# Batches with 528 slots: the sixteen tail tokens laid twice in each head's 32 rows, one pass for the tail's context

## The chip, the core and the metric

The kernel runs on one core of one Trainium2 chip (trn2). The metric is the device time of one execution in microseconds (us). Before the change the runs took 1044.05 us in the median (three runs: 1043.74, 1044.05 and one of 5687.53 us, which the median leaves out of account).

The core has five engines that run side by side and wait for each other by semaphores: TensorE (PE in the profile; its weight loads are listed apart as PEld), VectorE (DVE), ScalarE (ACT), GpSimd (POOL) and SyncE (SP), which here only issues transfers.

## The reference

One attention layer with a residual, 16 batches of 512 channels by 1024 tokens, 8 heads of 64 channels. Query, key and value are the same projection `q`. `mask` holds 0 or 1 for each token.

```python
xt = jnp.transpose(x, (0, 2, 1))
q = xt @ Wq.T
qh = q.reshape(B, T, NH, dk).transpose(0, 2, 1, 3)
scores = scale * jnp.einsum('bhqd,bhkd->bhqk', qh, qh)
logits = (scores * cmask + (1.0 - cmask) * NEG) * rmask
attn = jax.nn.softmax(logits, axis=-1)
ctx = jnp.einsum('bhqk,bhkd->bhqd', attn, qh)
ctx = ctx.transpose(0, 2, 1, 3).reshape(B, T, D)
out = ctx @ Wo.T
return x + jnp.transpose(out, (0, 2, 1))
```

A token with mask 0 gets no weight as a key (`cmask`), and as a query its logits are all 0 (`rmask`), so that its context is the mean of `q` over all tokens. Only the tokens with mask 1, a little over half of the 1024, need attention among themselves.

## The kernel before

**Slots.** For each batch the kernel puts the tokens with mask 1 into the first of `A` slots and gathers their rows of `x` by an indirect transfer on POOL's queue. `A` is fixed by the batch's rank (L64): 544 for batches 0 to 4, 528 for batches 5 to 13, 512 for the last two; batches 2 to 15 are taken in falling order of their number of such tokens. Slots 0 to 511 are four tiles of 128. What lies above 512 is the tail: 32 slots, 16 slots or none. Empty slots hold zeros, and their share is taken off the softmax sums afterwards.

**Precision by parts.** Values are cut into a high and a low part, and products are formed from the parts: in fp16 for the projections and scores, in fp32r (a reduced format of fp32 that TensorE takes) for the tail's context.

**Query and spread.** `query` (L497) projects into `q`; `qsplit` (L516) cuts a 128-channel chunk, that is two heads, into `hl` (high, low, high again) on DVE and lets SP's queue spread it by four transfers into `xx` (L536 to L539), where the parts of each head lie side by side. `hl` and `xx` are 544 slots wide; where `A` is 528, a memset (L525) puts zeros into the last 16 slots of `hl`.

**Scores and context.** For a head pair (`p`, four of them) and a key tile (`i`, four of them) `scores` (L653) forms the products of the tile's keys with all `A` queries into PSUM, four matmuls (L693) for each of two heads, and ACT takes the exponential into `p` (L697). `attend` (L702) multiplies these by the values `v` and accumulates over the key tiles in one PSUM tile `pav` (L718).

**The tail.** For the keys above 512 four heads share one tile: head `r` of the four lies in rows 32r to 32r+31, one row for each tail slot. `scores` with `i` None (L662 to L687) forms their products (L668), the exponential (L672), a high and a low part of it in fp32r (L677, L678), and spreads these by transfers into `pt`: for a head pair `pt` holds the high parts in 64 rows and the low parts of the same two heads in the other 64. The values come from `tail_copy` (L572), which repeats the tail's slots of `q` for the four row groups in `qt`, and `value_tail` (L580), which transposes `qt`, clears what belongs to the other head, and splits it into high (`t[:, 0]`, L597 on ACT) and low (`t[:, 1]`, L598 on DVE). With 16 tail slots rows 16 to 31 of each group are zero (a memset on POOL, L577, clears them once). `attend` with `i` 4 (L721, L722) then makes two passes over `pav` for each of the two column halves, high values and low values, four matmuls for a head pair. Since `pt` holds the high and the low exponentials in different rows, the two passes form all four products of parts. ACT then copies `pav` to `c` (L726).

**Order.** `run` (L925) writes out a list of steps (`S`: sixteen pairs of `p` and `i`, and two tail scores) for each batch and fills between them, by costs written at each step, the next batch's projection, transposes and values and the last batch's normalization and output projection (L809). A scheduler then orders the instructions of each engine by estimated times and priorities; each engine takes its instructions in that order.

Of the kernel before, what the change touches and what calls it, by code (L numbers as in the profile page):

```python
# [10 lines left out]
F32 = mybir.dt.float32  # L11
F32R = mybir.dt.float32r
F16 = mybir.dt.float16
I32 = mybir.dt.int32
AF = mybir.ActivationFunctionType
ALU = mybir.AluOpType
AX = mybir.AxisListType
PS = bass.MemoryType.PSUM

P = 128  # L20
# [10 lines left out]
C = 544  # L31
CT = C - 512
CQ = C + 2
HG = H // 2
# [12 lines left out]
class Fast:  # L47
# [91 lines left out]
    def setup2(self):  # L139
        nc, fixed = self.nc, self.fixed  # L140

        self.quad = fixed("quad", [P, HG])
        nc.vector.tensor_reduce(self.quad, self.ident.rearrange("p (r t) -> p r t", r=HG), AX.X, ALU.add)
        self.xh = fixed("xh", [P, DC, CQ], F16)
        self.xl = fixed("xl", [P, DC, CQ], F16)
        for t in (self.xh, self.xl):
            nc.gpsimd.memset(t[:, :, C + 1:], 0.0)

        self.rcol = [fixed("rcol%d" % k, [P, P]) for k in range(2)]
        self.smcol = [fixed("smcol%d" % k, [P, P]) for k in range(2)]  # L150
        for t in self.rcol + self.smcol:
            nc.gpsimd.memset(t, 0.0)

        self.two = fixed("two", [P, DK], F16)
        nc.vector.tensor_tensor(self.two, self.ident[:, :DK], self.ident[:, DK:], ALU.add)

        self.big = fixed("big", [P, self.B + 2 * DC])

        self.par = fixed("par", [P, 2])
        nc.vector.tensor_tensor(self.par, self.quad[:, 0:2], self.quad[:, 2:4], ALU.add)  # L160

    def load(self, name, c, half=None, after=None):

        if name not in self.w:
            self.w[name] = tuple(self.fixed("w" + name + k, [P, DC, D], F16) for k in "hl")
        cols = slice(0, D) if half is None else slice(half * D // 2, (half + 1) * D // 2)
        raw = self.sb([P, D], F32, "xa", 13)[:, cols]
        self.once(self.nc.sync.dma_start(out=raw, in_=self.src[name][c * P:(c + 1) * P, cols]), after)
        self.raw[name, c, half] = raw, cols

    def split(self, name, c, half=None):
        nc = self.nc
        raw, cols = self.raw[name, c, half]
        hi, lo = (w[:, c, cols] for w in self.w[name])
        nc.scalar.activation(hi, raw, AF.Copy, scale=SW)
        nc.vector.scalar_tensor_tensor(lo, raw, SW, hi, ALU.mult, ALU.subtract)
# [339 lines left out]
    def qsplit(self, b, e):  # L516


        nc, s = self.nc, self.st[b]
        A = s["A"]  # L520
        S = max(A, C) if A > 512 else A
        q = s["q"][:, e, :A]
        full = self.sb([P, 3, C], F16, "hl", 2)
        if A < S:
            nc.vector.memset(full[:, :, A:], 0.0)  # L525
        hl = full[:, :, :A]
        nc.vector.tensor_copy(hl[:, 0, :], q)
        nc.vector.tensor_tensor(hl[:, 1, :], q, hl[:, 0, :], ALU.subtract)
        nc.vector.tensor_copy(hl[:, 2, :], hl[:, 0, :])
        hl = full[:, :, :S]  # L530
        full = self.sb([P, 4, C], F16, "xx", 5)
        xx = full[:, :, :S]

        def spread():
            lo, up = slice(0, DK), slice(DK, P)
            nc.sync.dma_start(out=xx[lo, 0:2, :], in_=hl[lo, 0:2, :])  # L536
            nc.sync.dma_start(out=xx[up, 0:2, :], in_=hl[lo, 1:3, :])
            nc.sync.dma_start(out=xx[lo, 2:4, :], in_=hl[up, 0:2, :])
            self.last_xx = nc.sync.dma_start(out=xx[up, 2:4, :], in_=hl[up, 1:3, :]).ins  # L539

        self.later(spread)
        s["xx"].append(xx)
# [29 lines left out]
    def tail_copy(self, b, g):  # L572

        s = self.st[b]
        n = s["A"] - 512
        if g == 0 and b and s["A"] < self.wide[b - 1]:
            self.nc.gpsimd.memset(self.qt[:, :, :, n:], 0.0)  # L577
        self.nc.scalar.copy(self.qt[:, :, :, :n], s["q"][:, 2 * g:2 * g + 2, 512:512 + n].unsqueeze(2).broadcast_to([P, 2, HG, n]))

    def value_tail(self, b, g):  # L580


        nc, s = self.nc, self.st[b]
        if g == 0:
            s["vt"] = []
            s["sdt"] = self.sb([P, H], F32, "sdt")
        q = self.qt
        pv = self.pm([P, 2, P])
        for k in range(2):
            nc.tensor.transpose(pv[:, k, :], q[:, k].rearrange("p r t -> p (r t)"), self.ident)  # L590
        v = self.sb([P, HG, DK], F32, "tmp", 2)
        split = lambda t: t.rearrange("p (k h) d -> p k h d", h=2)
        nc.vector.tensor_tensor(split(v), pv.rearrange("p k (h d) -> p k h d", h=2),
                                self.par.unsqueeze(1).unsqueeze(3).broadcast_to([P, 2, 2, DK]), ALU.mult)
        self.squares(v, s["sdt"][:, HG * g:HG * g + HG], g == (b > 0), b == 0)
        t = self.sb([P, 2, HG, DK], F32R, "vt", 3)
        nc.scalar.copy(t[:, 0], v)  # L597
        nc.vector.tensor_tensor(t[:, 1], v, t[:, 0].bitcast(F32), ALU.subtract)  # L598
        s["vt"].append(t)

    def shift(self, b, g):
# [100 lines left out]
    def attend(self, b, p, i, ps):  # L702
        nc, s = self.nc, self.st[b]
        A = s["A"]
        CH = A // 2

        if i == 3:
            s["pav"] = self.ps_av.tile([P, 2, 512], F32, tag="av", name="pav")
        for g in range(2):
            for k in (1, 0) if i < 4 else range(2):  # L710
                cols = slice(g * CH, (g + 1) * CH)
                if i < 4:
                    with ExitStack() as st:
                        if self.group_first:

                            st.enter_context(self.behind(self.group_first))
                            st.enter_context(self.tc.high_priority(offset=HPO))
                        mm = nc.tensor.matmul(s["pav"][k * DK:(k + 1) * DK, g, :CH], lhsT=s["v"][p][:, i, k * DK:(k + 1) * DK],  # L718
                                              rhs=ps[k][:, cols], start=(i == 3), stop=(i == 0 and A == 512))
                    self.group_first = self.group_first or mm.ins  # L720
                elif A > 512:  # L721
                    nc.tensor.matmul(s["pav"][:, g, :CH], lhsT=s["vt"][p // 2][:, k, p % 2 * 2:p % 2 * 2 + 2, :],  # L722
                                     rhs=s["pt"][:, p % 2, cols], start=False, stop=(k == 1))
        if i == 4:
            c = self.sb([P, C], F32, "c", 4)
            nc.scalar.copy(c[:, :A].rearrange("p (g c) -> p g c", g=2), s["pav"][:, :, :CH])  # L726
            s["c"].append(c)
# [197 lines left out]
    def run(self, flag):  # L925
        B = self.B
        L = lambda f, *a: lambda: f(*a)
        S = [(p, i) for p in range(NP) for i in range(4)]
        S.insert(2, (0, None))
        S.insert(13, (1, None))  # L930
        N = len(S)
# [363 lines left out]
```

## Time and profile before

| what | value |
|---|---|
| median of the runs | 1044.05 us |
| the profiled execution's own time | 1045.58 us |
| its span (first to last instruction) | 1043.8 us |
| mean granted TensorE clock | 0.995 |
| exponentials of the 528-slot batches (5 to 13) | from about 350 us to about 912 us |

The profile is of one execution. A group's "busy" is the time in which at least one instruction of the group ran; matmuls overlap each other, so busy divided by the count is less than the mean duration of one. "Idle before" is the time that the engine sat idle right before instructions of the group, with what ended it. In the timeline, rows are merged runs of like instructions: the first column is the start, the second the length.

### The profile page before, as it was taken

The numbers are of one execution on the slowest core, as the hardware profiler recorded it, in microseconds if no ns is written. First come the engines' busy times: TensorE is split into PE (matmuls) and PEld (weight loads), VectorE is DVE, ScalarE is ACT, GpSimd is POOL, SyncE is SP. The second block draws the span as 40 slices with busy tenths as digits, with TensorE's granted clock in tenths as the row PEclk, the third lists the DMA queues.
The fourth block names the chain that finished last, engine by engine and source line by source line (L and its number), as shares of the span: only waits on it lengthen the run. The fifth ranks groups of instructions, "written<-read, shape, count | busy, mean of one in ns | idle before, by whom it ended". The sixth has DMA issues, their size and how long they took to land. (4 is left out here: it accounts for less than half of the span.)

```text
span 1043.8 us, 23675 instructions
## 1 busy us (share of the span) xinstructions
PE 994.7 (95%) x8527; PEld 692.3 (66%) x8527; DVE 720.9 (69%) x2408; ACT 656.4 (63%) x1702; POOL 299.5 (29%) x308
## 2 busy tenths in 40 slices
PE   7798999999999999999999999999999999999995
PEld 6576667666666766667676666766767676776552
DVE  7897668666766657767666777667678675756562
ACT  5876666666666665757666557665766666655650
POOL 3101023223301222233222223223333322325652
PEclk9899999999999999999999999999999999999999
DMA  6756555557645576666558656565665566546641
GB/s 212 215 142 175 138 152 166 164 156 207 189 125 149 135 214 176 166 189 163 164 159 233 183 141 188 152 192 175 202 193 153 164 172 183 154 132 195 201 170 74
DMA packets 78796, 177.74 MB, mean 170 GB/s; under 512 B 14688, under 2 KB 20576, under 8 KB 78672
## 3 DMA queue, kind: packets, MB, share of 16 engines
q1 hardware_dynamic: 57584, 108.40, 38.3%
q0 software_dynamic: 21088, 67.75, 20.7%
q8 instruction: 70, 1.15, 0.5%
q14 instruction: 54, 0.44, 0.1%
HBM read 91.49 MB, written 33.91 MB: 120 GB/s over the span
## 5 line engine op out<-in xcount | busy, mean ns | idle before, releaser
L697 ACT ACTIVATE p<-pss,nm 128x528 f32<-128x528 f32 (+2 forms) x512 | 359.9, 707 | 190.6 <-PE pss L693 181.1
L693 PE MATMUL pss<-xx 128*128 128x264 f16 (+2 forms) x2048 | 302.7, 277 | 8.2 <-ACT p L697 7.0
L718 PE MATMUL pav<-p,v 128*64 128x264 f32 (+2 forms) x2048 | 243.3, 390 | 0.0
L693 PEld LDWEIGHTS <-xx 128*128 128x128 f16 x2048 | 195.0, 99 | 63.9 <-issue 26.8
L718 PEld LDWEIGHTS pav<-p,v 128*64 128x64 f32 x2048 | 141.4, 137 | 85.7 <-issue 13.3
L893 POOL DMA_INDIRECT y_out<-xa,idx x68 | 73.7, 1083 | 284.7 <-PE pss L693 129.4
L508 PE MATMUL pm<-xh,wqh 128*128 128x264 f16 (+5 forms) x512 | 142.4, 278 | 4.1 <-DVE xa L814 2.3
L508 PE MATMUL pm<-xl,wqh 128*128 128x264 f16 (+5 forms) x512 | 141.7, 277 | 0.2 <-DVE xl L440 0.2
L508 PE MATMUL pm<-xh,wql 128*128 128x264 f16 (+5 forms) x512 | 141.9, 277 | 0.0
L390 POOL DMA_INDIRECT xa<-x_in,idx x68 | 67.9, 998 | 203.1 <-PE pss L693 89.6
L508 PEld LDWEIGHTS <-wqh 128*128 128x128 f16 x1024 | 98.1, 99 | 24.5 <-issue 7.5
L697 ACT ACTIVATION_READ_ACCUMULATOR p<-pss,nm 128x1 f32 x512 | 104.1, 203 | 0.0
L893 POOL DMA_INDIRECT y_out<-xi,idx x60 | 71.5, 1192 | 101.4 <-PE pss L693 38.1
L809 PE MATMUL pm<-woh,ch 128*128 128x512 f16 x240 | 91.1, 379 | 0.0
L809 PE MATMUL pm<-woh,cl 128*128 128x512 f16 x240 | 90.9, 379 | 0.0
L809 PE MATMUL pm<-wol,ch 128*128 128x512 f16 x240 | 90.9, 379 | 0.0
L390 POOL DMA_INDIRECT xi<-x_in,idx x60 | 61.7, 1029 | 97.3 <-PE pss L693 33.8
L511 ACT ACTIVATE q<-pm 128x264 f32<-128x264 f32 (+5 forms) x128 | 50.3, 393 | 60.1 <-PE pm L508 59.8
L809 PEld LDWEIGHTS <-ch 128*128 128x128 f16 x480 | 45.9, 98 | 44.7 <-issue 0.9
L814 DVE SCALAR_TENSOR_TENSOR xa<-pm,xa 128x512 f32<-128x512 f32 x60 | 41.3, 688 | 44.3 <-PE pm L809 40.6
L880 DVE TENSOR_TENSOR xi<-xi,ub 128x512 f32<-128x512 f32 (+1 forms) x60 | 40.7, 687 | 44.2 <-PE pss L693 41.7
L791 DVE TENSOR_TENSOR c<-c,rb 128x528 f32<-128x528 f32 (+2 forms) x64 | 45.4, 710 | 32.8 <-PE pm L508 16.3
(220 smaller groups left out, 1511.4 us busy)
## 6 DMA issues: line engine op xcount, KB each, us to landing
xx<-hl SPq DMA_DIRECT2D x224, 136.0 KB
xm<-x_nat_in SPq DMA_DIRECT2D x56, 512.0 KB
rb<-rd SPq DMA_DIRECT2D x72, 132.0 KB
rb<-rd SPq DMA_DIRECT2D x40, 136.0 KB
pt<-c SPq DMA_DIRECT2D x36, 132.0 KB
pt<-p SPq DMA_DIRECT2D x36, 132.0 KB
ub<-ud SPq DMA_DIRECT2D x16, 256.0 KB
xx<-hl SPq DMA_DIRECT2D x32, 128.0 KB
```

The source lines that it names most:

```text
L390: dma = self.nc.gpsimd.indirect_dma_start(out=tile[:n], out_offset=None, in_=self.x, in_offset=bass.IndirectOffsetOnAxis(ap=idx, axis=0))
L508: self.beat = nc.tensor.matmul(pq, lhsT=w[:, c, e * P:(e + 1) * P], rhs=xx[:, c, cols], start=(k == 0), stop=(k == 3 * DC - 1)).ins
L511: nc.scalar.activation(s["q"][:, e, cols], pq, AF.Copy, scale=1.0 / (SX * SW))
L693: self.beat = nc.tensor.matmul(pt[:, g, :CH], lhsT=xx[:, 2 * k, i * P:(i + 1) * P], rhs=xx[:, 2 * k + a, g * CH:(g + 1) * CH], start=(a == ...
L697: self.exp = [nc.scalar.activation(t.rearrange("p (g c) -> p g c", g=2), pt[:, :, :CH], AF.Exp, bias=s["nm"][p // HG][:, p % HG:p % HG + 1 ...
L718: mm = nc.tensor.matmul(s["pav"][k * DK:(k + 1) * DK, g, :CH], lhsT=s["v"][p][:, i, k * DK:(k + 1) * DK], rhs=ps[k][:, cols], start=(i == ...
L791: self.once(nc.vector.tensor_tensor(c[:, :A], c[:, :A], s["rb"][p], ALU.mult), self.beat if p < 3 else None)
L809: nc.tensor.matmul(po[:cols.stop - cols.start], lhsT=a[:, e, cols], rhs=w[:, e, :], start=(e == 0 and k == 0), stop=(e == DC - 1 and k == 2))
L814: self.nc.vector.scalar_tensor_tensor(x, po, 1.0 / (SX * SW), x, ALU.mult, ALU.add)
L880: self.once(self.nc.vector.tensor_tensor(x[:n], x[:n], s["ub"][:n], ALU.add), self.beat)
L893: dma = self.nc.gpsimd.indirect_dma_start(out=self.out, out_offset=bass.IndirectOffsetOnAxis(ap=idx, axis=0), in_=x, in_offset=None)
```

## The change

In batches with 528 slots the tail's 16 tokens are laid twice in each head's 32 rows, where the second 16 rows held zeros.

- `setup2` makes two columns of constants on DVE, once: `low`, which is 1 in the second half of every 32 rows and else 0, and `sign`, which is -1 there and else 1.
- `qsplit` copies slots 512 to 527 of `hl` to slots 528 to 543, after the three instructions that fill `hl`, in place of the memset ahead of them.
- `tail_copy` fills all of `qt`, eight repeats of 16 slots in place of four, and needs no memset on POOL.
- `value_tail` puts the high part, with `sign`, into `t[:, 1]`, and into `t[:, 0]` the high part in the first copy's rows and the low part in the second copy's.
- `attend` makes one pass with `t[:, 0]` in place of two: two matmuls for a head pair in place of four.

Batches with 544 and 512 slots keep their instructions.

```diff
@@ setup2
+        self.low = fixed("low", [P, 1])
+        nc.vector.tensor_reduce(self.low, self.ident.rearrange("p (r k t) -> p k r t", r=HG, k=2)[:, 1], AX.XY, ALU.add)
+        self.sign = fixed("sign", [P, 1])
+        nc.vector.tensor_scalar(self.sign, self.low, -2.0, 1.0, ALU.mult, ALU.add)
@@ qsplit
-        S = max(A, C) if A > 512 else A
         q = s["q"][:, e, :A]
         full = self.sb([P, 3, C], F16, "hl", 2)
-        if A < S:
-            nc.vector.memset(full[:, :, A:], 0.0)
         hl = full[:, :, :A]
         nc.vector.tensor_copy(hl[:, 0, :], q)
         nc.vector.tensor_tensor(hl[:, 1, :], q, hl[:, 0, :], ALU.subtract)
         nc.vector.tensor_copy(hl[:, 2, :], hl[:, 0, :])
-        hl = full[:, :, :S]
-        full = self.sb([P, 4, C], F16, "xx", 5)
-        xx = full[:, :, :S]
+        S = C if A > 512 else A
+        if A < S:
+            nc.vector.tensor_copy(full[:, :, A:], full[:, :, 512:A])
+            hl = full
+        xx = self.sb([P, 4, C], F16, "xx", 5)[:, :, :S]
@@ tail_copy
-        if g == 0 and b and s["A"] < self.wide[b - 1]:
-            self.nc.gpsimd.memset(self.qt[:, :, :, n:], 0.0)
-        self.nc.scalar.copy(self.qt[:, :, :, :n], s["q"][:, 2 * g:2 * g + 2, 512:512 + n].unsqueeze(2).broadcast_to([P, 2, HG, n]))
+        r = P // n
+        self.nc.scalar.copy(self.qt.rearrange("p k r t -> p k (r t)").rearrange("p k (r t) -> p k r t", t=n),
+                            s["q"][:, 2 * g:2 * g + 2, 512:512 + n].unsqueeze(2).broadcast_to([P, 2, r, n]))
@@ value_tail
-        nc.scalar.copy(t[:, 0], v)
-        nc.vector.tensor_tensor(t[:, 1], v, t[:, 0].bitcast(F32), ALU.subtract)
+        if s["A"] == C:
+            nc.scalar.copy(t[:, 0], v)
+            nc.vector.tensor_tensor(t[:, 1], v, t[:, 0].bitcast(F32), ALU.subtract)
+        else:
+            nc.scalar.activation(t[:, 1], v, AF.Copy, scale=self.sign)
+            nc.vector.scalar_tensor_tensor(t[:, 0], v, self.low, t[:, 1].bitcast(F32), ALU.mult, ALU.add)
@@ attend
-            for k in (1, 0) if i < 4 else range(2):
+            for k in (1, 0) if i < 4 else range(2 if A == C else 1):
...
-                                     rhs=s["pt"][:, p % 2, cols], start=False, stop=(k == 1))
+                                     rhs=s["pt"][:, p % 2, cols], start=False, stop=(k == 1 or A < C))
```

## The prediction

> **What bounds the kernel now.** I read the page first: the busy shares and the clock.
>
> ```profile
> span 1043.8 us, 23675 instructions
> PE 994.7 (95%) x8527; PEld 692.3 (66%) x8527; DVE 720.9 (69%) x2408; ACT 656.4 (63%) x1702; POOL 299.5 (29%) x308
> PE   7798999999999999999999999999999999999995
> PEclk9899999999999999999999999999999999999999
> ```
>
> TensorE is busy 95% of the span, and from the fifth slice to the last but one 90% or more of each; the next engine has 69%. A busy TensorE may still be waiting inside its pipeline, so I looked next at who waits for whom: the page's costliest groups and the table of waits.
>
> ```profile
> L697 ACT ACTIVATE p<-pss,nm 128x528 f32<-128x528 f32 (+2 forms) x512 | 359.9, 707 | 190.6 <-PE pss L693 181.1
> L693 PE MATMUL pss<-xx 128*128 128x264 f16 (+2 forms) x2048 | 302.7, 277 | 8.2 <-ACT p L697 7.0
> PE pss L693 <- ACT p L697: 7.0, 15, 0.8
> ```
>
> ScalarE's exponentials wait 181.1 us for TensorE's scores; the scores wait 7.0 us for the exponentials, never over 0.8 us at once. The wait lies on ScalarE's side, so TensorE's stream sets the pace. The changed batches run from about 350 to 912 us; a table by windows of 90 us, from which the first row and the sum of six, shows this stage alone.
>
> ```profile
> 380.00:470.00 90.00, 87.77 (x776) 61.05 (x775) 67.26 (x239) 56.41 (x146) 27.05 (x26) 1.00 0.62 177
> sum 540.00, PE 526.72 PEld 369.76 DVE 384.13 ACT 347.80 POOL 160.06; mean PE 87.79 PEld 61.63 DVE 64.02 ACT 57.97 POOL 26.68
> ```
>
> The granted clock there is 1.00. TensorE is busy 526.72 of 540 us (97.5%), VectorE 384.13 (71%), ScalarE 347.80 (64%). What leaves TensorE's stream here should leave the time, as long as nothing else becomes late.
>
> **The change part by part: TensorE.** There are 9 batches with 528 slots, each with 4 head pairs, and each pair loses 2 of its 4 tail matmuls: 72 go. The profile's group by shape has the 144 that stand there now, and the timeline shows what a run of four, and a run of one, cost in the stream.
>
> ```profile
> L722 PE MATMUL pav<-pt,vt 128*128 128x264 f32 x144 | 27.0, 306 | 0.0
> 469.16 0.73 PE L722 MATMUL pav<-pt,vt 128*128 128x264 f32 x4
> 469.74 0.41 PE L565 MATMUL pm<-two,xx 128*128 128x64 f16 x8
> 436.41 0.37 PE L722 MATMUL pav<-pt,vt 128*128 128x264 f32 x1
> 436.62 0.39 PE L809 MATMUL pm<-woh,ch 128*128 128x512 f16 x1
> ```
>
> The duration of one (306 ns) is no price, since matmuls overlap. From the start of four to the start of what follows is 469.74 - 469.16 = 0.58 us; of one, 436.62 - 436.41 = 0.21 us. So the first costs 0.21 us, with the change of number format, and each further one (0.58 - 0.21) / 3 = 0.123 us. The change takes two further ones and keeps the first: 72 x 0.123 = 8.9 us. The bound above is the group's busy time per matmul, 27.0 / 144 = 0.188 us, as if the pipeline stood empty around each: 72 x 0.188 = 13.5 us. The bound below is 0. I take 8.9, since it is the stream's own spacing. The Trainium skill, "TensorE: Matmul & The Clock Gate", section on the back-to-back issue gap, gives N / 2.4 + 2.5 ns for warm matmuls, 112.5 ns for 264 columns, and the sum would be 8.1 us by that estimate; the trace's 123 ns is a little slower and decides.
>
> Does all of it reach the time? TensorE is idle 540 - 526.72 = 13.3 us of this stage (2.5%), where others are late, and a shorter stream makes them a little later. I take a tenth off: 8.9 x 0.9 = 8.0 us.
>
> **ScalarE, VectorE and GpSimd.** These rows are the nearest to the changed operations.
>
> ```profile
> L578 ACT COPY qt<-q 128x128 f32<-128x128 f32 x18 | 5.5, 307 | 6.6 <-DVE q L514 6.4
> L578 ACT COPY qt<-q 128x256 f32<-128x256 f32 x10 | 4.1, 415 | 0.7 <-DVE q L514 0.7
> L697 ACT ACTIVATE p<-pss,nm 128x528 f32<-128x528 f32 x288 | 201.8, 705 | 112.3 <-PE pss L693 107.3 <-PE pav L718 2.3 <-issue 0.2
> L726 ACT COPY c<-pav 128x528 f32<-128x528 f32 x36 | 21.5, 596 | 0.0
> L525 DVE MEMSET hl<- 128x24 uint32 x36 | 2.8, 78 | 3.6 <-DMA xx<-hl 3.6
> L790 DVE COPY c<-mq 128x16 f32<-128x16 f32 x36 | 6.3, 176 | 6.3 <-DMA xx<-hl 6.2
> L529 DVE COPY hl<-hl 128x528 f16<-128x528 f16 x36 | 10.8, 299 | 0.0
> L577 POOL MEMSET qt<- x1: 205/205/205, 285.5 to 285.5; 128x128 f32 x1
> ```
>
> `tail_copy` now writes 256 columns in place of 128: 18 x (415 - 307) ns = 1.9 us on ScalarE. The split of the values takes its scale from a column of memory; nothing shows a copy of that form, and the nearest row is the exponential with its bias column beside a plain copy of as many columns, 705 - 596 = 109 ns, so between 0 and 18 x 109 ns = 2.0 us. Together up to 3.9 us, taken as nothing: the exponentials of these batches wait 107.3 us for TensorE. Without that cover it would be 3.9 us.
>
> On VectorE 36 memsets of 78 ns become copies of 3 x 16 elements. The nearest row, a copy of 16 columns, has 176 ns; a copy of 528 has 299 ns and bounds it. That is 36 x 98 ns = 3.5 us (at most 36 x 221 ns = 8.0 us) on an engine with 29% to spare. The low part becomes a three-operand instruction; on VectorE this costs the same where the trace has both:
>
> ```profile
> L440 DVE SCALAR_TENSOR_TENSOR xl<-pm,xh 128x512 f16<-128x512 f32 x60 | 38.7, 683 | 26.5 <-ACT xh L439 26.3
> L528 DVE TENSOR_TENSOR hl<-q,hl 128x512 f16<-128x512 f32 x8 | 5.5, 688 | 0.1
> 15.22 0.69 DVE L440 SCALAR_TENSOR_TENSOR xl<-pss,xh 128x512 f16<-128x512 f32 x1 [0.99 <-ACT xh L439]
> L622 DVE TENSOR_REDUCE m<-pm 128x1 f32<-128x128 f32 x32 | 9.1, 283 | 3.3 <-PE pm L620 2.2
> L631 DVE TENSOR_SCALAR nm<-pm 128x4 f32<-128x4 f32 x32 | 4.9, 154 | 15.9 <-PE pm L629 15.2
> ```
>
> 683 against 688 ns: nothing. The two constants are one small reduction (at most 283 ns) and one small scaling (154 ns), some 0.44 us, queued before the first input splits; VectorE stands idle for 0.99 us right ahead of the first of those (15.22 us), so they cost nothing, and 0.44 us if that gap is taken. The memset on GpSimd (0.2 us, once) saves nothing: GpSimd is not on the path.
>
> **The added wait.** The first of the four transfers of `xx` needed the low part (L528); it now needs the copy that stands behind L529 as well.
>
> ```profile
> 470.23 0.71 DVE L528 TENSOR_TENSOR hl<-q,hl 128x528 f16<-128x528 f32 x1
> 470.86 0.29 DVE L529 COPY hl<-hl 128x528 f16<-128x528 f16 x1
> 471.01 0.48 SPq L536 DMA_DIRECT2D xx<-hl  x1
> 472.82 0.59 SPq L539 DMA_DIRECT2D xx<-hl  x1
> 482.03 0.41 PE L565 MATMUL pm<-two,xx 128*128 128x64 f16 x8
> ```
>
> L528 ends at 470.94 and the issue starts at 471.01; L529 ends at 471.15, and with 0.18 us for the copy the issue would start 0.4 us later. Behind it on SP's queue stand the other three, then rows of reciprocals (`rd`, `rb`), `pt` and the next loads of `x`. TensorE takes this `xx` for the values at 482.03, 9.2 us after the last of the four was issued, so the 0.4 us is hidden. Were it on the path for all 36 chunks, it would cost 14.4 us.
>
> **The sum.** 8.0 us less, nothing added: the span goes from 1043.8 to 1035.8 us, the profiled execution's own time from 1045.58 to 1037.6. The median of the runs lies 1.5 us below the profiled execution, so the forecast is 1044.05 - 8.0 = 1036.0 us.
>
> **The rivals.** *The stream shortens and the time doesn't.* If TensorE's busy time hides pipeline waits, what was late stays late. For it: weight loads fill only 369.76 of the 540 us, and there are 13.3 us of plain idleness. Against it: the exponentials' 107.3 us of waiting for TensorE. It would give 1044, and with a part of the gain anything from 1040. The Trainium skill's "Perfetto Trace Analysis", section on identifying the most-contended engine, speaks for this rival: matmul busy time is a poor measure of how full TensorE is, and the share of weight loads (here 68%) a better one; by that rule TensorE has a third to spare. The waits of this trace don't agree with it as a measure of what bounds.
>
> *More than the spacing goes.* If each removed matmul costs what the group's busy time shows, because its fp32r weights load slowly, 13.5 us go: 1030.5 us.
>
> ```profile
> L722 PEld LDWEIGHTS pav<-pt,vt x224: 186/190/192, 56.2 to 918.4; 128*128 128x128 f32 x112
> ACT corr L642 <- DVE nm L634: 19.3, 10, 6.6
> 622.28 0.27 PE L508 MATMUL pm<-xh,wqh 128*128 128x266 f16 x1 [1.19 <-DVE nm L631]
> ```
>
> For it: a load takes 190 ns, over the 123 ns of spacing. Against it: in the run of four the loads plainly overlap.
>
> *Slower.* The scheduler places ScalarE's instructions anew. In the changed program the small exponential `corr` (L642) stands one or two places earlier in ScalarE's queue in six places in batches 4 to 11, ahead of a projection's copy or of a score's exponential. It waits for a chain that goes VectorE, TensorE, VectorE, and holds what is queued behind it: 19.3 us in ten cases now, the longest 6.6 us, where TensorE lost only 1.19 us. At 1.19 us each six cost 7.1 us and the gain is nearly gone; at 6.6 us each, 39.6 us: 1044 - 8.0 + 39.6 = 1076 us. The point from which it decides is when the wait outlasts the two score tiles that TensorE can fill ahead, about two exponentials, 1.4 us (2 x 705 ns). Slower than before needs more than 8.0 / 6 = 1.3 us of TensorE's time at each place. Against it: 19.3 us over ten waits means that most of them are short, and the scores wait for the exponentials only 7.0 us in all as it is.
>
> **How the numbers follow.** The forecast, 1033 to 1040: 0.76. No or little gain, 1040 to 1045: 0.12. The larger gain, about 1030.5: 0.06. Slower than before, 1045 to 1076: 0.06, of which a third lies above 1065. The range for 8 in 10 holds the forecast and takes in an unhidden 3.9 us on ScalarE and half of the second case: 1032 to 1042 us. Over 2% (20.9 us, about what a measurement of this kernel can tell from no change) faster means under 1023.2 us, below even the larger gain: 0.02. Over 2% slower means above 1064.9 us: 0.02. Within 2%: 0.96.
>
> **What would show it.** The step on TensorE: 72 instead of 144 tail matmuls of 264 columns, about 14 us of busy time for the group, and runs of two with 0.33 us to the next start. The step to the time: TensorE's busy time falls by about 9 us, the span by 8, and the exponentials still wait for TensorE. The hidden work: the copy of 256 columns at 415 ns in all 28 places, the cast with a scale column under 530 ns, the new copy near 0.18 us, and no wait of L565 or L668 for `xx`. The forecast is wrong if TensorE's idle time in the stage grows by what it lost in busy time (the first rival), if the waits of `corr` grow beyond 19.3 us and TensorE's scores wait for the exponentials well over 7.0 us (the slower one), or if the span falls by over 11 us.

## The result, and the profile after

The changed kernel takes 1036.29 us in the median (eight runs, 1033.31 to 1038.75), the kernel before 1043.89 us in the runs beside it. The ratio is 0.9931, with a 95% interval of 0.9915 to 0.9947: 7.2 us less (0.69% of 1043.89), between 5.5 and 8.9, and within 2%, as forecast. The ratio leaves out the run of 5687.53 us and is not the quotient of the two medians, which lie 7.6 us apart. Two later groups of runs, each on one chip together with the kernel before, gave 0.9923 [0.9900, 0.9946] and 0.9939 [0.9919, 0.9959] for the same kernel. The profiled execution took 1036.56 us.

First the page of the changed kernel: span, busy time of the engines, and the slices of TensorE and its clock.

```profile
span 1034.9 us, 23506 instructions
PE 989.3 (96%) x8455; PEld 686.2 (66%) x8455; DVE 724.1 (70%) x2410; ACT 659.2 (64%) x1702; POOL 301.5 (29%) x307
PE   7798999999999999999999999999999999999996
PEclk9899999999999999999999999999999999999998
```

The span fell by 8.9 us (1043.8 - 1034.9), with 72 matmuls fewer (8527 - 8455). TensorE's busy time fell by 5.4 us, VectorE's and ScalarE's rose by 3.2 and 2.8 us. TensorE is as full as before. The costliest groups, the sum of the six windows of 90 us between 380 and 920 us, and the table of waits of the changed kernel say the same:

```profile
L705 ACT ACTIVATE p<-pss,nm 128x528 f32<-128x528 f32 (+2 forms) x512 | 359.3, 706 | 186.5 <-PE pss L701 176.6
L701 PE MATMUL pss<-xx 128*128 128x264 f16 (+2 forms) x2048 | 302.7, 277 | 6.3 <-ACT p L705 5.2
```

```profile
sum 540.00, PE 526.80 PEld 367.68 DVE 392.75 ACT 354.36 POOL 165.46; mean PE 87.80 PEld 61.28 DVE 65.46 ACT 59.06 POOL 27.58
```

```profile
ACT p L705 <- PE pss L701: 176.6, 109, 3.5
ACT corr L650 <- DVE nm L642: 19.2, 10, 4.4
PE pss L701 <- ACT p L705: 5.2, 12, 0.6
PE pav L730 <- DMA pt<-p: 4.4, 4, 2.2
```

(L705 is the exponential that was L697, L701 the scores that were L693, L650 the `corr` that was L642, L730 the tail's context that was L722.) The scores still wait for the exponentials only 5.2 us, the exponentials for the scores 176.6 us, 4.5 less than before, and TensorE is busy 526.80 of 540 us where it was 526.72. So TensorE went on as the bound, with a shorter stream. One row is worse: the tail's context waits for the spread exponentials (`pt`) four times, 4.4 us in all, where in the kernel before it waited once, 2.2 us:

```profile
PE pav L722 <- DMA pt<-p: 2.2, 1, 2.2
```

To see where the 8.9 us of the profiled span lie, I cut the span at the first exponential of batch 5 and the first of batch 14, and added up, within this stage, the time from each matmul's start to the next one's:

| from starts of matmuls (us) | before | after | difference |
|---|---|---|---|
| up to the stage | 350.12 | 351.10 | +1.0 |
| the stage (batches 5 to 13) | 561.55 | 554.84 | -6.7 |
| from the stage to the last matmul | 122.16 | 121.00 | -1.2 |
| after the last matmul | 9.96 | 7.92 | -2.0 |
| in the stage: tail matmuls (L722, then L730) | 21.25 | 12.18 | -9.1 |
| sums of 64 columns over keys (L565, L569) | 9.45 | 10.76 | +1.3 |
| tail scores (L668, L676) | 10.20 | 10.78 | +0.6 |
| scores (L693, L701), with the waits of what follows them | 144.78 | 146.45 | +1.7 |
| projections (L508, L513) | 98.70 | 97.32 | -1.4 |

The parts outside the stage, which hold two of the 72 removed matmuls, are otherwise not the change's: the 9.96 us after the last matmul are 7.7 to 8.4 us in every later profile, one of a kernel with all 144 tail matmuls among them. Nor is the last row: most of it is a single wait (620.82 to 622.28 us, 1.35 us longer than a usual start) of the profile before, which that kernel doesn't have either. What belongs to the stage is 9.1 us out, 1.9 us back behind the tail (1.3 + 0.6), and 1.7 us more in the row of the scores. Of the idle times in the stage, that ahead of the tail's context rose from none to 2.2 us, and that of the scores for the exponentials fell from 2.1 to 1.0 us; these waits vary from one execution to the next, as the experiments show. The timeline of TensorE shows the 9.1 us and the first part of what came back. In the kernel before the stretch at 469.16 us stands in the prediction; the later one goes on so (start, length, operation and number of merged instructions):

```profile
481.46 0.73 PE L722 MATMUL pav<-pt,vt 128*128 128x264 f32 x4
482.03 0.41 PE L565 MATMUL pm<-two,xx 128*128 128x64 f16 x8
482.37 0.63 PE L668 MATMUL pss<-xx 128*32 128x264 f16 x16
```

and in the changed kernel:

```profile
469.03 0.48 PE L730 MATMUL pav<-pt,vt 128*128 128x264 f32 x2
469.36 0.41 PE L569 MATMUL pm<-two,xx 128*128 128x64 f16 x8
...
481.13 0.49 PE L730 MATMUL pav<-pt,vt 128*128 128x264 f32 x2
481.46 0.46 PE L569 MATMUL pm<-two,xx 128*128 128x64 f16 x8
481.90 0.63 PE L676 MATMUL pss<-xx 128*32 128x264 f16 x16
```

The tail run takes 0.33 us to the next start (469.36 - 469.03, and 481.46 - 481.13) where four took 0.57 (482.03 - 481.46). But at the second place the eight narrow matmuls behind it take 0.44 us to the next start (481.90 - 481.46) where they took 0.34 (482.37 - 482.03): 0.24 us were won and 0.10 given back at once.

### The profile page after: what moved, and what is told of

Same layout as the page of the kernel before. It is cut to its first block, busy times and chain, and to the rows that moved or that the text cites. A ratio compares the mean times of both kernels' runs of the same rounds, so it can differ in the third digit from the quotient of the medians.

```text
span 1034.9 us, 23506 instructions
## 1 busy us (share of the span) xinstructions
PE 989.3 (96%) x8455; PEld 686.2 (66%) x8455; DVE 724.1 (70%) x2410; ACT 659.2 (64%) x1702; POOL 301.5 (29%) x307
## 5 line engine op out<-in xcount | busy, mean ns | idle before, releaser
L705 ACT ACTIVATE p<-pss,nm 128x528 f32<-128x528 f32 (+2 forms) x512 | 359.3, 706 | 186.5 <-PE pss L701 176.6
L701 PE MATMUL pss<-xx 128*128 128x264 f16 (+2 forms) x2048 | 302.7, 277 | 6.3 <-ACT p L705 5.2
L701 PEld LDWEIGHTS <-xx 128*128 128x128 f16 x2048 | 194.9, 99 | 64.2 <-issue 26.2
L726 PEld LDWEIGHTS pav<-p,v 128*64 128x64 f32 x2048 | 141.5, 137 | 85.6 <-issue 13.5
L513 PE MATMUL pm<-xh,wqh 128*128 128x264 f16 (+5 forms) x512 | 142.4, 278 | 3.7 <-DVE xa L822 3.1
L513 PE MATMUL pm<-xh,wql 128*128 128x264 f16 (+5 forms) x512 | 141.9, 277 | 0.0
L513 PE MATMUL pm<-xl,wqh 128*128 128x264 f16 (+5 forms) x512 | 141.8, 277 | 0.0
L513 PEld LDWEIGHTS <-wqh 128*128 128x128 f16 x1024 | 98.3, 99 | 23.7 <-issue 7.1
L705 ACT ACTIVATION_READ_ACCUMULATOR p<-pss,nm 128x1 f32 x512 | 104.1, 203 | 0.0
L901 POOL DMA_INDIRECT y_out<-xi,idx x60 | 73.6, 1226 | 96.7 <-PE pss L701 27.6
```

What stands on the lines that cost most here:

```text
L513: self.beat = nc.tensor.matmul(pq, lhsT=w[:, c, e * P:(e + 1) * P], rhs=xx[:, c, cols], start=(k == 0), stop=(k == 3 * DC - 1)).ins
L701: self.beat = nc.tensor.matmul(pt[:, g, :CH], lhsT=xx[:, 2 * k, i * P:(i + 1) * P], rhs=xx[:, 2 * k + a, g * CH:(g + 1) * CH], start=(a == ...
L705: self.exp = [nc.scalar.activation(t.rearrange("p (g c) -> p g c", g=2), pt[:, :, :CH], AF.Exp, bias=s["nm"][p // HG][:, p % HG:p % HG + 1 ...
L901: dma = self.nc.gpsimd.indirect_dma_start(out=self.out, out_offset=bass.IndirectOffsetOnAxis(ap=idx, axis=0), in_=x, in_offset=None)
```

## Experiments

The kernels ran in three groups: the first four (one, two and four passes, and the added copy four times over) on one chip, where the kernel before took 1052.83 us; the next four on a second (1044.00 us), and the last three on the second again (1045.33 us). Times are compared through the ratio to the kernel before on the same chip. The theory: the 72 removed matmuls are worth their place in TensorE's stream, 0.123 us each, a tenth off, and all that is added hides. The rivals are those of the prediction.

### One pass alone, without what makes it exact

Against the kernel before:

```diff
-            for k in (1, 0) if i < 4 else range(2):
+            for k in (1, 0) if i < 4 else range(2 if A == C else 1):
...
-                                     rhs=s["pt"][:, p % 2, cols], start=False, stop=(k == 1))
+                                     rhs=s["pt"][:, p % 2, cols], start=False, stop=(k == 1 or A < C))
```

> The kernel before with the second tail pass left out in the batches with 528 slots and nothing else changed; it leaves the low part of the tail's values out of the context. My theory (the gain is the 72 matmuls' place in TensorE's stream, 0.123 us each): 1044 - 8.0 = 1036, at most 2 us below the changed kernel, whose added copy and waits this one hasn't got. Rival (the gain comes from the new instructions' order or from the memsets' removal): 1042 to 1045.

It took 1047.26 us, 0.9936 [0.9921, 0.9951] of the kernel before: the change's gain within the interval, without any of the change's additions. In the stage the tail matmuls take 12.20 us, as in the changed kernel, and the sums and tail scores behind them rise by the same 1.3 and 0.6 us. So the gain, and that part of what is given back, come from the shorter pass, not from the doubled slots.

### Everything of the change, with the second pass kept

Against the changed kernel:

```diff
-            for k in (1, 0) if i < 4 else range(2 if A == C else 1):
+            for k in (1, 0) if i < 4 else range(2):
...
-                                     rhs=s["pt"][:, p % 2, cols], start=False, stop=(k == 1 or A < C))
+                                     rhs=s["pt"][:, p % 2, cols], start=False, stop=(k == 1))
```

> The changed kernel with its second tail pass put back (the signed high parts of the two copies cancel, so the pass adds zero). All that the change added stands, the 72 matmuls stand too. My theory: as the kernel before, 1044, up to 3 us above it where the later transfers of the tail's exponentials hold TensorE. Rival (order or other parts carry the gain): as the changed kernel, 1036.

It took 1051.55 us, 0.9983 [0.9970, 0.9996]. Nearly the whole gain is gone, and what the change adds on the other engines costs nothing that can be seen. The tail matmuls take 21.31 us of the stage again (before 21.25), and the rows of the sums and the tail scores are back at 9.46 and 10.19 us. By the ratio it is 0.4 to 3.2 us faster than before; I have no cause for that.

### Four passes

Against the changed kernel:

```diff
-            for k in (1, 0) if i < 4 else range(2 if A == C else 1):
+            for k in (1, 0) if i < 4 else range(2 if A == C else 4):
...
-                    nc.tensor.matmul(s["pav"][:, g, :CH], lhsT=s["vt"][p // 2][:, k, p % 2 * 2:p % 2 * 2 + 2, :],
-                                     rhs=s["pt"][:, p % 2, cols], start=False, stop=(k == 1 or A < C))
+                    nc.tensor.matmul(s["pav"][:, g, :CH], lhsT=s["vt"][p // 2][:, min(k, 1), p % 2 * 2:p % 2 * 2 + 2, :],
+                                     rhs=s["pt"][:, p % 2, cols], start=False, stop=(k == (1 if A == C else 3)))
```

> The changed kernel with four passes in place of one in the batches with 528 slots; the three added ones cancel or double only the signed high parts of both copies, which add up to zero. 216 matmuls more than the changed kernel. My theory, a stream that is full: 216 x 0.123 = 26.6 us above it, 1063, and 144 x 0.123 = 17.7 above two passes. Rival (TensorE's busy time hides slack): clearly less, under 1055.

It took 1070.78 us, 1.0182 [1.0158, 1.0207]. The group of the tail matmuls by shape, in the kernels with one, two and four passes (busy us, mean ns of one, idle before):

```profile
L730 PE MATMUL pav<-pt,vt 128*128 128x264 f32 x72 | 17.6, 326 | 2.2 <-DMA pt<-p 2.2
```

```profile
PE 999.9 (95%) x8527; PEld 695.6 (66%) x8527; DVE 724.5 (69%) x2410; ACT 660.2 (63%) x1702; POOL 298.1 (28%) x307
...
L730 PE MATMUL pav<-pt,vt 128*128 128x264 f32 x144 | 27.1, 307 | 1.5 <-DMA pt<-p 1.5
```

```profile
PE 1014.7 (95%) x8671; PEld 711.2 (67%) x8671; DVE 725.1 (68%) x2410; ACT 662.2 (62%) x1702; POOL 300.3 (28%) x307
...
L730 PE MATMUL pav<-pt,vt 128*128 128x264 f32 x288 | 44.5, 295 | 0.0
```

From 144 to 288 the group's busy time rises by 17.4 us, TensorE's by 14.8 us, and the medians by 19.2 us (1070.78 - 1051.55); the last is 0.134 us for each of the 144, with some 3 us of uncertainty on the whole by the two intervals (by the ratios the difference is 0.0199 of 1052.83, 21.0 us). By the starts of the matmuls it is 0.121 us each: 38.26 - 21.31 = 16.95 us for the 140 of them that lie in the stage. The time follows the number of tail matmuls, down and up, so nothing else in the stage hides them. This refutes the rival in which the stream shortens and the time doesn't. The larger gain falls as well: at 0.188 us each, 144 matmuls would cost 27.0 us. The Trainium skill, "Perfetto Trace Analysis", section on identifying the most-contended engine, names the share of weight loads, beside the operations done as a share of the peak, as the measure of how close TensorE is to its limit. That share was two thirds in all these kernels (66 to 67%), while the time followed the number of matmuls; so here the share of weight loads alone didn't tell what a matmul more or less does to the time.

### The added copy four times over

Against the changed kernel:

```diff
-            nc.vector.tensor_copy(full[:, :, A:], full[:, :, 512:A])
+            for _ in range(4):
+                nc.vector.tensor_copy(full[:, :, A:], full[:, :, 512:A])
```

> The changed kernel with the new copy of 16 slots made four times in a row, so that the spread of the projected chunk waits some 0.3 to 0.5 us more, and what stands behind it on the transfer queue as well. If that wait is hidden, as the prediction has it: 1036 and 1037, within 1.5 us of the changed kernel. Rival (the added wait already costs, by the tail's exponentials that queue behind it and reach TensorE late): 3 us or more above the changed kernel, with more idle time at the tail's matmuls.

It took 1044.40 us, 0.9906 [0.9887, 0.9925]: not slower than the changed kernel, although three more copies stand between the low part and the first transfer of `xx` in each of 36 chunks. By the ratios it is even 2.6 us faster than the changed kernel on its own chip, which is outside the 1.5 us expected, on the other side; the second run didn't show that again. In this run, next to the changed kernel on one chip:

> The added copy four times over, now on the same chip as the changed kernel. If the wait that the copy adds ahead of the transfers is hidden, the ratio lies within 0.003 of the changed kernel's. If each 0.17 us counts for all 36 chunks, three more copies cost 18 us and the ratio is 0.017 above.

1038.54 us, 0.9927 [0.9899, 0.9955], against 1037.87 us and 0.9939 for the changed kernel. The medians differ by 0.7 us, where 18 us would follow if every chunk paid. The wait that the copy adds is hidden, at four times its length too. The copies by their group, and SP's wait for them, in the first run:

```profile
L535 DVE COPY hl<-hl 128x48 f16<-128x48 f16 x144 | 26.0, 180 | 1.7
```

```profile
SPq L541 <- DVE hl L535: 54.5, 25, 3.8
```

The queue that issues the transfers waited 54.5 us for the last copy in 25 places. In the changed kernel it waited 42.2 us for the one copy, also in 25 places, so each wait grew by some 0.5 us, and the medians show none of it.

### The waits for `pt`

Of the changed kernel's four waits for `pt` three lie in the stage, 2.2 us of idle time in all; the longest, at 88.66 us, lies ahead of it, as does the only one of the kernel before, at 87.75 us. In the changed kernel's timeline one of the three looks so:

```profile
405.35 0.61 PE L701 MATMUL pss<-xx 128*128 128x264 f16 x4
406.79 0.48 PE L730 MATMUL pav<-pt,vt 128*128 128x264 f32 x2 [0.83 <-DMA pt<-p]
407.12 0.29 PE L513 MATMUL pm<-xh,wqh 128*128 128x266 f16 x1
```

`pt` is issued behind the four transfers of `xx` on SP's queue, and the change makes those wait longer; that this causes the wait was my guess. Two edits put it to the test: the copy of the tail's slots put ahead of the third part's copy, so that it covers the high and low parts only and the first transfer no longer stands behind the third part's copy; and the transfers of `pt` given the scheduler's high priority.

The copy early, against the changed kernel:

```diff
-        nc.vector.tensor_copy(hl[:, 2, :], hl[:, 0, :])
         S = C if A > 512 else A
         if A < S:
-            nc.vector.tensor_copy(full[:, :, A:], full[:, :, 512:A])
+            nc.vector.tensor_copy(full[:, :2, A:], full[:, :2, 512:A])
             hl = full
+        nc.vector.tensor_copy(hl[:, 2, :], hl[:, 0, :])
```

> The changed kernel with the copy of the 16 slots made ahead of the third part's copy, on two parts (the third then copies all 544 columns), so that the first transfer of the spread needs less: about 0.3 us earlier on the transfer queue. If the later transfers cost the changed kernel time: up to 2 us below it. If they are hidden: the same within 1 us.

It took 1032.95 us, 0.9900 [0.9874, 0.9926]. The changed kernel ran beside it:

> The changed kernel once more, on the chip on which the variants above run, as their measure: a ratio of 0.993 to the kernel before, within its interval of 0.9915 to 0.9947.

1036.30 us, 0.9923 [0.9900, 0.9946]. The difference, 3.4 us, is more than the 2 us expected, but the intervals overlap, so both ran again with more runs:

> The kernel with the copy of the tail's slots ahead of the third part's copy, once more with more runs, beside the changed kernel and the one with four copies. If the order of the copy is worth something (the low part's wait ends earlier), its ratio stays near 0.990 and the changed kernel's near 0.993, with intervals apart. If the difference was the scatter from run to run (the changed kernel's own runs span 5.4 us), the two ratios agree within 0.002.

> The changed kernel a third time. The ratio to the kernel before stays between 0.9915 and 0.9947, as in the first comparison, by either theory.

The copy early: 1034.37 us, 0.9898 [0.9875, 0.9922]; the changed kernel: 1037.87 us, 0.9939 [0.9919, 0.9959]. It was the fastest kernel of both groups, by 3.4 and 3.5 us. The intervals, which hold the scatter of the kernel before as well, still touch (0.9922 over 0.9919); but in the last group the slowest of its six runs (1035.29 us) lies below the fastest of the changed kernel's eight (1036.38 us). So I take the 3 us as likely; their cause is open.

The traces don't settle whether the waits for `pt` are that cause. Their idle time in the stage is 2.2, 0.8 and 2.5 us in the three profiles of the changed kernel and 1.5 us with two passes. It is nothing in the kernel before, 0.5 us with one pass alone, and nothing and 1.2 us with the copy early. That points to the added copy, as my guess has it. But with four copies, where the guess asks for longer waits, it is 1.0 and 1.9 us. The waits vary from one execution to the next, and what sets them is open.

The transfers of `pt` first, against the changed kernel:

```diff
-                    nc.sync.dma_start(out=s["pt"][half[k], k, :].bitcast(F32), in_=hi[half[k]].bitcast(F32))
-                    nc.sync.dma_start(out=s["pt"][half[1 - k], k, :].bitcast(F32), in_=lo[half[k]].bitcast(F32))
+                    with self.tc.high_priority(offset=HPO):
+                        nc.sync.dma_start(out=s["pt"][half[k], k, :].bitcast(F32), in_=hi[half[k]].bitcast(F32))
+                        nc.sync.dma_start(out=s["pt"][half[1 - k], k, :].bitcast(F32), in_=lo[half[k]].bitcast(F32))
```

> The changed kernel with the transfers of the tail's exponentials (pt) at a higher priority, so that on the transfer queue they go ahead of the spread of the projected chunk where both are ready. My theory: the shorter stream brings TensorE to the tail pass before these transfers have landed (3.2 us of waits of 0.1 to 1.3 us in the changed kernel's profile, in the stage of the 528-slot batches); without these waits 1 to 3 us below the changed kernel. Rival (the waits only take the place of others, or the chunk's spread becomes late in turn): the same or slower.

It took 1048.45 us, 1.0049 [1.0029, 1.0069]: slower than the kernel before. Its table of waits:

```profile
PE pm L513 <- DVE nm L639: 6.6, 4, 2.2
...
PE pm L569 <- DMA xx<-hl: 2.6, 4, 1.2
PE pav L731 <- DMA pt<-p: 1.6, 2, 0.8
```

The wait for `pt` did fall, from 4.4 to 1.6 us, but the projections now wait 6.6 us for `nm` (a column of VectorE's that the exponentials need) and the sums 2.6 us for `xx`. The stage took 569.23 us, 14.4 more than the changed kernel's, of which the projections hold 8.4 and the output projection 4.3. The priority moved more than the four transfers. What removing the wait for `pt` alone is worth was therefore not measured. Both edits together:

> Both: the copy ahead of the third part's copy and the tail's exponentials first on the transfer queue. If both effects are there: 1 to 4 us below the changed kernel; else the same.

1046.80 us, 1.0028 [1.0005, 1.0051]: the early copy doesn't mend it.

## Why the prediction was right, step by step

**TensorE is the bound, and its stream sets the time.** Right, and shown: one pass alone gives 0.9936, keeping the second pass gives 0.9983, doubling it 1.0182.

**72 matmuls at 0.123 us, 8.9 us.** Right, and a little low. The stage lost 9.07 us for the 70 removed matmuls that lie in it, 0.130 each; over the whole profile the starts of the tail matmuls of 264 columns fall from 21.45 to 11.92 us, 9.5 us for all 72. The group's busy time for one matmul, 0.188 us, was the wrong price, as argued. One of its signs was wrong: about 14 us of busy time was expected for the group, half of 27.0, and 17.6 us was measured. The first matmul of each run keeps its full length, so the group loses only the further ones at the stream's price (27.0 - 8.9 = 18.1 us would have followed from the prediction's own sum).

**A tenth off.** The size came out about right (0.9 us expected; the comparisons leave 0 to 3.4 of the 8.9 us off), but the reason didn't hold, so that was luck. I had argued that others' lateness would take it, and TensorE's idle time in the six windows stayed at 13.2 us (13.3 before). The account shows 1.9 us given back by TensorE itself, in the sums and tail scores right behind the shorter pass, in every kernel with one pass and in none with two or four. So the forecast of 8.0 us stands for 9.5 out and 1.9 back, 7.6 us: two terms were too small, and they nearly cancel. TensorE's busy time fell by 5.4 us and not by about 9. The 1.9 us count as busy; the rest, 2.2 us, is in part the scatter of profiles, as the fall is 5.9 and 6.5 us in the changed kernel's two other profiles and 7.1 us from the kernel with two passes to that with one pass alone. For what is left I have no row.

**ScalarE.** Right. The cast with its scale column and the copy of 256 columns, by their lines in the changed kernel (count, then shortest, median and longest in ns, then the first and last start):

```profile
L605 ACT ACTIVATE vt<-tmp,sign x18: 510/514/526, 317.1 to 846.8; 128x256 fp32r<-128x256 f32 x18
```

```profile
L581 ACT COPY qt<-q x28: 396/412/438, 27.9 to 841.6; 128x256 f32<-128x256 f32 x28
```

and the cast before, without a scale column:

```profile
L597 ACT CAST vt<-tmp x28: 390/412/449, 28.1 to 852.8; 128x256 fp32r<-128x256 f32 x28
```

The scale column costs 514 - 412 = 102 ns; the bound was 109. The Trainium skill, "ScalarE: Activation LUTs", section "What ACT_TABLE_LOAD costs", has about 93 ns for each column operand of an activation, and the trace agrees within a tenth. The cost is hidden: in the kernel with two passes kept it is all there, and the time isn't above that of before.

**VectorE.** The new copy was expected near 0.18 us and took 0.174. The three-operand instruction was expected to cost nothing more, and here a term was mis-sized:

```profile
L534 DVE COPY hl<-hl x36: 165/174/177, 303.2 to 841.8; 128x48 f16<-128x48 f16 x36
```

```profile
L606 DVE SCALAR_TENSOR_TENSOR vt<-tmp,low,vt x18: 473/475/482, 317.8 to 847.8; 128x256 fp32r<-128x256 f32 x18
```

```profile
L598 DVE TENSOR_TENSOR vt<-tmp,vt x28: 409/416/419, 28.8 to 853.8; 128x256 fp32r<-128x256 f32 x28
```

475 against 416 ns: 59 ns more, 1.1 us in 18 places. The pair of rows that I compared (683 and 688 ns) had fp16 results at 512 columns, and those were not near enough. It was hidden, like the rest. The two constants took 209 and 145 ns, 0.35 us where 0.44 was expected; VectorE still stood idle, for 1.31 us, ahead of the first split behind them (0.99 before), so they held nothing up.

**The added wait.** Right: the sums (L569) wait for no `xx`, the tail scores (L676) only at about 40 us, ahead of the changed batches, as they did before, and four copies were hidden too. One step is missing: I named `pt` among what is queued behind these transfers and worked out the slack of the sums alone. The waits for `pt` rose from 2.2 to 4.4 us in the profile, all of it in the stage; that the added copy raised them is not shown.

**The rivals.** The one without gain needed TensorE's idle time to grow; it stayed at 13.2 of 540 us. The larger gain is refuted by the prices above, and 13.5 us lies outside all three intervals of the changed kernel (at most 10.4 us, 0.9900). The slower one needed longer waits of `corr`: 19.2 us in ten places against 19.3, the longest 4.4 us against 6.6, and the scores waited 5.2 us for the exponentials against 7.0. Its places in the queue moved, and nothing came of it.

## What to carry to other kernels

Price a removed matmul by the distance of starts in the stream of the engine that sets the time, not by the group's busy time or by one instruction's length; and check it with a kernel that does the removal alone and one that doubles it. Whether an added wait is hidden is found out by making it several times as long. Raising the priority of a few transfers in a scheduled kernel reorders other engines too, so it is no test of those transfers alone.

## What the runs showed of the hardware

Behind a shorter run of fp32r matmuls the next matmuls took longer. Behind two of them instead of four, single starts of the 64-column matmuls (L569) lie 92 to 95 ns (eight times in the stage), 127 to 131 ns (six) or 168 to 172 ns (seven) apart where 29 ns is usual, in the changed kernel and with one pass alone. Before, and with two passes kept, there are nine longer ones, of 119 to 139 ns. This is 1.3 us in the stage, with another 0.6 us at the tail scores. In the stretch at 481.46 us the second weight load of these matmuls starts 67 ns after the first, where it was 15 ns at 482.03 us before, and the second matmul starts 31 ns after its load (28 ns before): it moved with its weight load. Why the load starts later is not shown; that the longer pass had covered it is likely and wasn't tried.

The runs of one kernel in one group on one chip lie up to 10.8 us apart (1045.22 to 1055.99 us with the transfers of `pt` first; 1036.38 to 1041.70 us for the changed kernel). One chip took 1052.83 us for the kernel before where another took 1044.00. The kernel with four copies left a profile on each of these two: 354.28 and 350.97 us up to the stage, 555.63 and 558.37 us in it, 126.54 and 120.88 us from it to the last matmul. So the slower chip lost its time outside the stage. Differences of 3 us, as the early copy's, need both kernels in the same group of runs.
